# The rows' reciprocal roots on ScalarE and VectorE instead of GpSimd, with the planner's due places refitted

## Chip, cores and metric

The kernel runs on one core of a Trainium2 chip. The metric is the time of one execution on the device in microseconds; lower is better. A core has a matrix engine (TensorE, "PE" in the profile, with its weight loads as "PEld"), VectorE ("DVE"), ScalarE ("ACT"), GpSimd ("POOL") and a queue for transfers on SyncE ("SP"). Each engine works through its own list of instructions in order; semaphores hold an instruction until what it needs is there.

## What is computed

The input is x of shape 32 x 128 x 64 x 64 (images, channels, height, width) in fp32. Two layers follow each other:

```
# layer 0: group norm (32 groups), a convolution in a learned butterfly basis, and a residual
x = x + conv(_gn(x), weight, kd1, kd2, k11, k12, k21, k22)
# layer 1, on tokens: each image gives 4096 rows of 128 channels
t = _to_tokens(x)
t = t + attn(_ln_t(t), Wk, bk, Wv, bv)          # softmax over channels, one 128 x 128 matrix per image
t = t + moe(_ln_t(t), router_w, router_b, expert_w, expert_b)   # 8 experts, the 2 best per row
x = _from_tokens(t, x)

def _ln_t(v, eps=1e-5):
    m = jnp.mean(v, axis=-1, keepdims=True)
    s = jnp.var(v, axis=-1, keepdims=True)
    return (v - m) / jnp.sqrt(s + eps)
```

So every row is normalized twice in layer 1, and each time a reciprocal root of its variance is needed: 4096 rows an image, held as a 128 x 32 tile (row in the partition, 32 groups of 128 rows).

## The kernel before

The kernel has three parts. The first normalizes by groups and takes each image into the transform basis; the second mixes channels for each frequency; the third, which the change touches, takes one image after the other through the inverse transform, the attention and the experts.

In the third part three images are in work at once: image b is transformed back ("conv"), image b - 1 goes through both norms and the attention ("front"), and image b - 2 through the experts ("experts"). The steps of an image, by the keys that the code uses:

- conv: eight "w" on PE (L877, tile pu, from one PSUM buffer pair "cv" in use at a time), each emptied by two "wo" on ACT (L887, two copies each, into u); four "h" on PE (L899, py), each added to the image by "ho" on DVE (L907, y). The first two images use smaller pieces (L920, L939).
- front: "pt" transposes on PE (L1021), copied by "to" on ACT (L1026, tk); "sa" row statistics on DVE (L993, bs); "va" moments on DVE (L1003 to L1008, m); **"pwa"**, the power (L1013, m<-m,mhalf); "na" two small DVE operations (L1050, L1051); "xg" normalized rows on ACT (L1061); "pg" Gram matrix on PE (L1072); a short softmax chain ("gs", "pb", "sm", "pr", "sr", "sn", "pc", "prx", L1085 to L1124, with an Exp on ACT at L1107); "pp" products on PE (L1145), scaled by "at" on ACT (L1158, L1162) and added by "ad" on DVE (L1173); then "vb" moments, **"pwb"**, the second power, "lg" first half of the routing logits on DVE (L1204 to L1208), "nb" two small DVE operations (L1212, L1213), and the choice of experts on DVE ("l2", "f1" to "f4", "gt", L1218 to L1248) with one small Exp on ACT ("f5", L1239).
- experts: "xn" normalized rows on ACT (L1273), "px" transposes on PE (L1283), "xT" copies on ACT (L1289), 64 "pe" on PE (L1296), each weighed by "m" on DVE (L1307, tm), summed by sixteen "s" on POOL (L1332, L1333, L1335, five instructions each), transposed back by "st" on PE (L1342, po), copied by "so" on ACT (L1348) and stored. In the last image five of the sixteen sums are made on DVE instead (L1319).

The order of the instructions is written by a planner, `Plan`, when the kernel is built. Each step is added with its engine, an assumed duration in us, a due place, the steps that it needs, and the buffers that it takes and frees. The planner then plays the steps through: whenever an engine is free, it takes the ready step with the earliest due place whose buffers are free. The order that comes out is the order of the instructions on each engine; on the chip nothing is reordered. The due place of a step is its slot, 114 us an image, plus an entry of the table `SHIFT` for its key with the digits taken off ("w3" and "w0" are "w", "t1" is "t", "l2" is "l"):

```
        at += SHIFT.get(key.rstrip("0123456789_"), 0.0)
        made[b, key] = plan.add(
            engine, us, SLOT * at, run, [made[k] for k in names if k[0] >= 0], take, free, late
        )
```

Among the buffers are 3 for "pe" (PSUM), 3 for "tl" (PSUM, shared by the transposes and products), 1 for "cv", 2 each for the image x, xn, xT and tm.

The power is one GpSimd instruction: the variance plus epsilon, 128 x 32 values, to the power -1/2, with a tile of -0.5 as exponent (`mhalf`). It is planned with 5.5 us. The group norm of the first part has a power of its own (L349), which the change leaves as it is.

Of the kernel before, what the change touches and what calls it, by code (L numbers as in the profile page):

```python
# [11 lines left out]
AF = mybir.ActivationFunctionType  # L12
ALU = mybir.AluOpType
# [77 lines left out]
def kernel(  # L91
# [15 lines left out]
    nc = tc.nc  # L107
# [47 lines left out]
    mhalf = cp.tile([P, NT], F32, name="mhalf")  # L155
# [7 lines left out]
    with ExitStack() as ph1:  # L163
        pp = ph1.enter_context(tc.tile_pool(name="pp1", bufs=4, space=PSUM))
        xp = ph1.enter_context(tc.tile_pool(name="xp1", bufs=3))
        st = ph1.enter_context(tc.tile_pool(name="st1", bufs=1))
# [9 lines left out]
        def add(key, engine, us, at, run, after=(), take=(), free=(), late=0.0):  # L176
            after = [made[k] for k in after if k in made]
            if engine == "PE":
                after += on_pe[-1:]
            made[key] = plan.add(engine, us, SLOT * at, run, after, take, free, late)  # L180
            if engine == "PE":
                on_pe.append(made[key])
# [342 lines left out]
        for s in range(B + 2):  # L525
            if s == 0:
                norm(2)
            for g in range(4):
                at = s + 0.25 * g
# [36 lines left out]
    with ExitStack() as ph2:  # L566
# [146 lines left out]
        for w in range(n):  # L713
# [9 lines left out]
            for half in range(2):  # L723
                for t in range(4):
                    at = w + 0.5 * half + 0.125 * t
# [42 lines left out]
    st = ctx.enter_context(tc.tile_pool(name="st", bufs=1))  # L768
# [16 lines left out]
    xg = [ct.tile([P, 4, P], F32, name=f"xg{i}") for i in range(NG)]  # L785

    QX = P + 2 * NE
    prx = [ct.tile([P, QX], F32, name=f"prx{i}") for i in range(2)]
# [10 lines left out]
    def prepare():  # L799
# [24 lines left out]
    SLOT = 114.0  # L824

    SHIFT = {
        "ad": -0.15, "at": -0.25, "f": 0.71, "gs": -1.97, "gt": 0.71, "h": -0.24, "ho": -3.5, "kvp": 3.43,
        "kvq": -0.45, "l": 0.71, "lg": 3.61, "m": -0.32, "na": -1.87, "nb": -0.81, "pb": -1.97, "pc": -1.97,
        "pe": 0.16, "pg": -0.08, "pp": 0.19, "pr": -1.97, "prx": -1.97, "pt": -0.23, "pwa": -1.87, "pwb": 3.61,
        "px": 0.15, "r": -0.04, "s": 0.08, "sa": 1.29, "sm": -1.97, "sn": -1.97, "so": 2.13, "sr": -1.97,  # L830
        "st": 1.1, "t": -1.97, "to": 0.06, "va": -1.87, "vb": 3.61, "w": 0.28, "x": -0.68, "xT": -0.68,
        "xg": 0.21, "xn": 2.42,
    }
    made = {}

# [150 lines left out]
    def front(b):  # L986

        t = tk[b % 2]
        v = {}
# [5 lines left out]
        def moments(which):  # L995

            bs = v["bs"]
            even, odd = bs[:, :, 0, :], bs[:, :, 1, :]
            m2 = st.tile([P, 6, NT], F32, name=f"m2{which}_{b}", tag=f"m2{which}", bufs=2)
            total, diff, var, nmr, rstd, above = (m2[:, k, :] for k in range(6))  # L1000
            if which == 1:
                v["above"] = above
            nc.vector.tensor_add(total, even[:, :, 1], odd[:, :, 1])  # L1003
            nc.vector.tensor_sub(diff, even[:, :, 1], odd[:, :, 1])
            nc.vector.tensor_add(var, even[:, :, 2], odd[:, :, 2])
            nc.vector.tensor_mul(diff, diff, diff)
            nc.vector.tensor_scalar(var, var, 1.0 / P, LN_EPS, ALU.mult, ALU.add)
            nc.vector.scalar_tensor_tensor(var, diff, 0.25, var, ALU.mult, ALU.add)  # L1008
            v[which] = total, var, nmr, rstd

        def power(which):
            total, var, nmr, rstd = v[which]
            nc.gpsimd.tensor_tensor(rstd, var, mhalf, ALU.pow)  # L1013

        def turn(g):
            def run():
# [22 lines left out]
        s1 = b + 1  # L1039
        for g in range(8):  # L1040
            at = s1 + 0.016 * g
            add(b, f"pt{g}", "PE", 0.48, at, turn(g), [(b - 2, f"st{g}")] + [f"ho{k}" for k in range(4)], ("tl",))
            add(b, f"to{g}", "ACT", 0.55, at, turned(g), [f"pt{g}"], (), ("tl",))
            add(b, f"sa{g}", "DVE", 0.85, at, stats1(g), [f"to{g}"] + (["sa0"] if g else []))
        add(b, "va", "DVE", 1.7, s1 + 0.14, lambda: moments(1), [f"sa{g}" for g in range(8)])
        add(b, "pwa", "POOL", 5.5, s1 + 0.14, lambda: power(1), ["va"])

        def nmr1():
            total, var, nmr, rstd = v[1]
            nc.vector.scalar_tensor_tensor(nmr, total, -0.5, rstd, ALU.mult, ALU.mult)  # L1050
            nc.vector.tensor_scalar_add(v["above"], nmr, 1.0)  # L1051

        add(b, "na", "DVE", 0.9, s1 + 0.14, nmr1, ["pwa"])


        def norm(g):
# [21 lines left out]
        for g in range(8):  # L1078
            at = s1 + 0.26 + 0.016 * g
# [46 lines left out]
        at = s1 + 0.40  # L1126
# [50 lines left out]
        for j, lo in enumerate(range(0, NT, 3)):  # L1177
            m = min(3, NT - lo)
            at = s1 + 0.45 + 0.016 * j
# [28 lines left out]
            nc.vector.tensor_add(lg, lg, eq)  # L1208

        def nmr2():  # L1210
            total, var, nmr, rstd = v[2]
            nc.vector.scalar_tensor_tensor(nmr, total, -0.5, rstd, ALU.mult, ALU.mult)  # L1212
            nc.vector.tensor_scalar_add(nmr, nmr, 1.0)  # L1213
            tile_of["norm", b] = rstd, nmr
# [35 lines left out]

        at = s1 + 0.64
        add(b, "vb", "DVE", 1.7, at, lambda: moments(2), [f"ad{lo}" for lo in range(0, NT, 3)])
        add(b, "pwb", "POOL", 5.5, at, lambda: power(2), ["vb"])
        add(b, "lg", "DVE", 1.95, at, logits1, ["vb"])
        add(b, "nb", "DVE", 2.1, at + 0.1, nmr2, ["pwb", "lg"])
        add(b, "l2", "DVE", 1.95, at + 0.1, logits2, ["nb"], ("gate",))
        add(b, "f1", "DVE", 4.15, at + 0.1, lambda: first_max(0), ["l2"])
        add(b, "f2", "DVE", 0.4, at + 0.1, second, ["f1"])
# [123 lines left out]
    for b in range(B):  # L1382
        transfers(b)
        conv(b)
        front(b)
        experts(b)
# [37 lines left out]
def build(arrays):  # L1424
    import concourse.bacc as bacc

    nc = bacc.Bacc("TRN2", target_bir_lowering=False, num_devices=1)
    args = [
        nc.dram_tensor(k, a.shape, mybir.dt.from_np(a.dtype), kind="ExternalInput").ap() for k, a in arrays.items()
    ]  # L1430
    shape = arrays["in_x_dram"].shape
    args.append(nc.dram_tensor("out_0_dram", shape, F32, kind="ExternalOutput").ap())
    with tile.TileContext(nc) as tc:
        kernel(tc, *args)
    return nc
# [8 lines left out]
```

## Time and profile before

| | |
|---|---|
| Time, median of 3 runs | 6059.13 us (6056.47 to 6059.99) |
| Span of the profiled execution | 6062.4 us; no other time of that execution is recorded |
| First and second part | to about 2530 us |
| Third part | from about 2590 us to the end |
| Instructions | 219265 |
| Mean granted TensorE clock | 0.991 of full speed |

"Busy" is the time in which an engine has an instruction at work; register, branch and semaphore instructions and DMA issues are not counted. Matmuls are pipelined and their ends are modelled, so a matmul that is recorded with 0.592 us may follow the one before it by 0.43 us: on PE the starts are to be compared. The chain of work that ended last is followed back from the last instruction, at each step to what released it. A wait is put down to the releaser that came last. In the list of groups and in the timeline, the bracket at the end of a line is the time that the engine idled before the instruction, and what ended it. A matmul in fp32 that the code writes once appears as two instructions, a transpose as one.

### The profile page before, as it was taken

Reading aid. Unit: us, or ns where it says so; the run is one execution under the profiler, and the core shown is the slowest. Engines: PE = TensorE matmul, PEld = TensorE weight load, DVE = VectorE, ACT = ScalarE, POOL = GpSimd, SP = SyncE. Lnnn points to the kernel's source line nnn. Section 1 sums busy time; section 2 is a strip of 40 time slices with the busy share of each in tenths; the row PEclk is TensorE's granted clock in tenths of the full one; section 3 lists DMA queues with packets and bytes.
Section 4 is the critical chain, followed back from the end, with each engine's and each line's share of the span. In section 5 each row is a group of like instructions: output and inputs, shape, how many; then the busy total and the mean of one; then the engine's idle time right before and its main releaser. Section 6 shows DMA issues by size and latency. Waiting matters only on the chain.

```text
span 6062.4 us, 219265 instructions
## 1 busy us (share of the span) xinstructions
PE 5891.6 (97%) x95372; PEld 4677.6 (77%) x95372; DVE 4221.2 (70%) x7696; ACT 3756.5 (62%) x7057; POOL 4191.0 (69%) x3765
## 2 busy tenths in 40 slices
PE   7999999999999999889999999999999999999998
PEld 7999999999999999776666666666666666666654
DVE  5565545555555555448878787787878878787878
ACT  7666664555555555366667667666766766676663
POOL 2110006666666666428898898989989898998988
PEclk9999999999999999999999999999999999999999
DMA  6767666666666666632313222231322223132100
GB/s 200 238 224 237 234 214 193 172 173 172 172 174 171 171 171 172 160 107 77 92 56 102 67 88 81 72 97 57 101 68 84 84 64 104 57 97 71 65 27 28
DMA packets 555044, 756.74 MB, mean 125 GB/s; under 512 B 58592, under 2 KB 319712, under 8 KB 549984
## 3 DMA queue, kind: packets, MB, share of 16 engines
q1 hardware_dynamic: 551856, 738.76, 41.0%
q8 instruction: 749, 12.27, 0.9%
q0 software_dynamic: 896, 2.62, 0.1%
q14 instruction: 215, 1.76, 0.1%
q10 hardware_dynamic: 1328, 1.32, 0.1%
HBM read 406.93 MB, written 335.54 MB: 122 GB/s over the span
## 4 chain that ended last, share of the span: by engine, by line
PE 88%; ACT 7%; issue 2%; DVE 1%; POOL 1%; DMA 1%; SPq 0%; ACTq 0%; POOLq 0%; DVEq 0%
PE pe L1296 28%; PE m L654 17%; PE g L632 9%; PE pf L418 7%; PE pu L877 6%; PE pp L1145 4%; PE py L899 4%; PE pg L1072 4%; PE pv L396 3%; PE px L1283 2%; ACT xn L1273 2%; ACT u L887 2%; PE pz L373 1%; PE pt L1021 1%; ACT z L383 1%
## 5 line engine op out<-in xcount | busy, mean ns | idle before, releaser
L1296 PE MATMUL pe<-ew_sb,xT 128*128 128x512 f32 x4096 | 1948.4, 597 | 18.6 <-DVE tm L1307 15.1
L1307 DVE TENSOR_TENSOR tm<-pe,oh 128x512 f32<-128x512 f32 x2028 | 1346.6, 684 | 478.9 <-PE pe L1296 456.6
L1332 POOL TENSOR_TENSOR tm<-tm 128x512 f32<-128x512 f32 x1014 | 1285.0, 1284 | 202.6 <-DVE tm L1307 199.3
L1296 PEld LDWEIGHTS pe<-ew_sb,xT 128*128 128x128 f32 x4096 | 701.6, 191 | 523.4 <-issue 400.1
L643 DVE COPY f<-g 128x1024 f32<-128x1024 f32 x508 | 622.3, 1225 | 644.4 <-PE g L632 644.2
L654 PE MATMUL m<-f,s 128*64 128x64 f32 x32768 | 1068.9, 224 | 1.1 <-ACT f L643 0.8
L654 PEld LDWEIGHTS m<-f,s 128*64 128x64 f32 x32768 | 999.0, 138 | 62.4 <-issue 1.5
L600 POOL COPY s<-l 128x512 f32<-128x512 f32 x512 | 547.2, 1105 | 526.4 <-issue 509.7
L643 ACT COPY f<-g 128x1024 f32<-128x1024 f32 x508 | 514.7, 1013 | 556.4 <-PE g L632 530.1
L1335 POOL TENSOR_TENSOR tk<-tk,tm 128x256 f32<-128x256 f32 x1014 | 753.9, 743 | 79.5
L1333 POOL TENSOR_TENSOR tm<-tm 128x512 f32<-128x512 f32 x507 | 650.3, 1283 | 39.8
L887 ACT COPY u<-pu 64x512 f32<-64x512 f32 x960 | 556.3, 579 | 135.1 <-PE pu L877 121.6
L632 PE MATMUL g<-c,wst 9*128 9x128 f32 x16256 | 599.6, 283 | 1.7 <-issue 1.5
L632 PEld LDWEIGHTS g<-c,wst 9*128 9x128 f32 x16256 | 503.0, 186 | 36.2 <-issue 1.5
L349 POOL TENSOR_TENSOR grstd<-gms,mhalf 128x1 f32<-128x1 f32 x32 | 17.8, 555 | 737.8 <-DVE gms L345 737.8
L1158 ACT ACTIVATE pp<-pp,m 128x128 f32<-128x128 f32 x1024 | 440.9, 431 | 124.2 <-PE pp L1145 99.2
L602 POOL TENSOR_SCALAR s<-l 128x512 f32<-128x512 f32 x256 | 511.3, 1997 | 0.0
L877 PEld LDWEIGHTS pu<-qw,r 128*128 128x128 f32 x3840 | 455.1, 193 | 62.8 <-ACT u L887 49.0
L877 PE MATMUL pu<-qw,r 128*128 128x128 f32 x3840 | 475.8, 277 | 25.1 <-ACT u L887 25.1
L1289 ACT COPY xT<-px 128x512 f32<-128x512 f32 x256 | 150.2, 587 | 563.2 <-PE px L1283 560.1
L418 PE MATMUL pf<-ph,v 128*128 128x128 f32 x4096 | 491.2, 278 | 6.2 <-issue 1.4
L418 PEld LDWEIGHTS pf<-ph,v 128*128 128x128 f32 x4096 | 467.0, 192 | 16.0 <-ACT z L383 7.1
(169 smaller groups left out, 8569.6 us busy)
## 6 DMA issues: line engine op xcount, KB each, us to landing
xf<-f SPq DMA_DIRECT2D x512, 256.0 KB, 3.3
pf<-o SPq DMA_DIRECT2D x1024, 128.0 KB, 3.3
l<-xf SPq DMA_DIRECT2D x1012, 128.0 KB, 3.2
r<-pf SPq DMA_DIRECT2D x504, 256.0 KB, 4.7
x<-in_x_dram SPq DMA_DIRECT2D x256, 256.0 KB, 4.5
y<-in_x_dram SPq DMA_DIRECT2D x32, 2048.0 KB, 9.3
out_dram<-so SPq DMA_DIRECT2D x256, 256.0 KB, 2.2
tw<-in_tw_dram SPq DMA_DIRECT2D x6, 384.0 KB, 7.5
```

The costliest lines, as they stand in the source:

```text
L418: nc.tensor.matmul(pl[:, j * P : (j + 1) * P], vs[b][:, 8 * g + j, :], ph.rearrange("h r m -> h (r m)"), start=True, stop=True,)
L600: nc.gpsimd.tensor_copy(dst, src)
L632: nc.tensor.matmul(pg[g // 2][:, g % 2, m * P : (m + 1) * P], wst[rows, 16 * half + 4 * t + m, :], c[rows].rearrange("r h k -> r (h k)"), ...
L643: copy(f.rearrange("i m (g o) -> i m g o", g=2), tile_of["g", w, half, t][k].rearrange("i g (o m) -> i m g o", o=4))
L654: nc.tensor.matmul(ps[hh * n : (hh + 1) * n, q, :], s[:, h].rearrange("i k b -> i (k b)")[:, B * r : B * r + n], f[:, h, r, :], start=(r = ...
L877: nc.tensor.matmul(ps[:, k, :], rs[b, e][:, k * P : (k + 1) * P], qw.rearrange("w r m -> w (r m)"), start=True, stop=True,)
L887: nc.scalar.copy(u[r * n : (r + 1) * n, :, oh * n + 8 * e : oh * n + 8 * e + 8], ps[oh * n : (oh + 1) * n, :, r * n : (r + 1) * n].rearran ...
L1296: nc.tensor.matmul(ps, tile_of["xT", b, i // 4][:, i % 4, :], ew_sb[:, es, :].rearrange("d e c -> d (e c)"), start=True, stop=True,)
L1307: nc.vector.tensor_tensor(tile_of["tm", b, i // 2][:, i % 2, es, :], tile_of.pop(("pe", b, i, half)).rearrange("p (e c) -> p e c", c=P), t ...
L1332: nc.gpsimd.tensor_tensor(tm[:, k, 0:4, :], tm[:, k, 0:4, :], tm[:, k, 4:8, :], ALU.add)
L1333: nc.gpsimd.tensor_tensor(tm[:, :, 0:2, :], tm[:, :, 0:2, :], tm[:, :, 2:4, :], ALU.add)
L1335: nc.gpsimd.tensor_tensor(t[:, lo : lo + 2, :], t[:, lo : lo + 2, :], tm[:, :, m, :], ALU.add)
```

## The change

Both powers of the third part leave GpSimd. In their place ScalarE takes the natural logarithm of the variance and then the exponential of -0.5 times it, and VectorE makes one Newton step on the result, three instructions, at the head of "na" and "nb". The planner's steps "pwa" and "pwb" become ACT steps of 0.55 us, "na" goes from 0.9 to 1.4 us and "nb" from 2.1 to 2.6. Every entry of SHIFT is new; two keys that no step uses are gone, and "wo" is added.

```
@@ SHIFT
-        "ad": -0.15, "at": -0.25, "f": 0.71, "gs": -1.97, "gt": 0.71, "h": -0.24, "ho": -3.5, "kvp": 3.43,
-        "kvq": -0.45, "l": 0.71, "lg": 3.61, "m": -0.32, "na": -1.87, "nb": -0.81, "pb": -1.97, "pc": -1.97,
-        "pe": 0.16, "pg": -0.08, "pp": 0.19, "pr": -1.97, "prx": -1.97, "pt": -0.23, "pwa": -1.87, "pwb": 3.61,
-        "px": 0.15, "r": -0.04, "s": 0.08, "sa": 1.29, "sm": -1.97, "sn": -1.97, "so": 2.13, "sr": -1.97,
-        "st": 1.1, "t": -1.97, "to": 0.06, "va": -1.87, "vb": 3.61, "w": 0.28, "x": -0.68, "xT": -0.68,
-        "xg": 0.21, "xn": 2.42,
+        "ad": -4.220, "at": -1.623, "f": 1.979, "gs": -2.122, "gt": 1.288, "h": -0.225, "ho": -2.066,
+        "l": -0.694, "lg": 13.929, "m": -3.037, "na": 2.809, "nb": 3.903, "pb": -3.699, "pc": -8.262,
+        "pe": 0.110, "pg": -1.062, "pp": 0.179, "pr": -1.382, "prx": -2.690, "pt": -0.071, "pwa": 3.358,
+        "pwb": -2.233, "px": 0.135, "r": 3.879, "s": 10.318, "sa": 8.276, "sm": -7.752, "sn": -3.975,
+        "so": -2.291, "sr": 8.801, "st": 0.395, "t": -1.530, "to": -11.017, "va": -4.512, "vb": 4.281,
+        "w": 6.698, "wo": 0.030, "x": -4.067, "xT": -6.105, "xg": 0.748, "xn": 3.218,
@@ front
         def power(which):
             total, var, nmr, rstd = v[which]
-            nc.gpsimd.tensor_tensor(rstd, var, mhalf, ALU.pow)
+            nc.scalar.activation(rstd, var, AF.Ln)
+            nc.scalar.activation(rstd, rstd, AF.Exp, scale=-0.5)
+
+        def newton(which):
+            total, var, nmr, rstd = v[which]
+            nc.vector.scalar_tensor_tensor(var, var, -0.5, rstd, ALU.mult, ALU.mult)
+            nc.vector.tensor_tensor(var, var, rstd, ALU.mult)
+            nc.vector.scalar_tensor_tensor(rstd, var, 1.5, rstd, ALU.add, ALU.mult)
...
-        add(b, "pwa", "POOL", 5.5, s1 + 0.14, lambda: power(1), ["va"])
+        add(b, "pwa", "ACT", 0.55, s1 + 0.14, lambda: power(1), ["va"])
         def nmr1():
+            newton(1)
...
-        add(b, "na", "DVE", 0.9, s1 + 0.14, nmr1, ["pwa"])
+        add(b, "na", "DVE", 1.4, s1 + 0.14, nmr1, ["pwa"])
...
         def nmr2():
+            newton(2)
...
-        add(b, "pwb", "POOL", 5.5, at, lambda: power(2), ["vb"])
+        add(b, "pwb", "ACT", 0.55, at, lambda: power(2), ["vb"])
...
-        add(b, "nb", "DVE", 2.1, at + 0.1, nmr2, ["pwb", "lg"])
+        add(b, "nb", "DVE", 2.6, at + 0.1, nmr2, ["pwb", "lg"])
```

## The prediction

> **What bounds the kernel now.** The profile page comes first: the busy shares, and the chain of work that ended last.
>
> ```profile
> PE 5891.6 (97%) x95372; PEld 4677.6 (77%) x95372; DVE 4221.2 (70%) x7696; ACT 3756.5 (62%) x7057; POOL 4191.0 (69%) x3765
> ...
> PE 88%; ACT 7%; issue 2%; DVE 1%; POOL 1%; DMA 1%; SPq 0%; ACTq 0%; POOLq 0%; DVEq 0%
> ```
>
> TensorE carries 88% of the chain and GpSimd 1%. These are means over stages, so next come the stretches of the last part, cut at the first transform matmul of an image (L899), which returns every 106.37 us: (5825.49 - 4017.26) / 17.
>
> ```profile
> core 0: us, PE busy (x) PEld busy (x) DVE busy (x) ACT busy (x) POOL busy (x), PEclk, DMA share, GB/s
> 2847.10:2953.50 106.40, 105.05 (x744) 71.82 (x743) 85.47 (x189) 72.91 (x168) 95.28 (x83) 1.00 0.26 80
> 5719.10:5825.50 106.40, 105.06 (x746) 71.85 (x747) 85.48 (x189) 73.05 (x168) 95.26 (x83) 1.00 0.11 41
> 5825.50:5931.90 106.40, 94.08 (x447) 56.68 (x448) 85.51 (x196) 58.95 (x148) 93.71 (x82) 0.94 0.05 20
> 5931.90:6062.00 130.10, 109.28 (x336) 53.02 (x334) 110.19 (x224) 39.95 (x94) 113.81 (x105) 0.94 0.09 33
> ```
>
> From 2847 to 5825 there are 28 equal slots, one image each: PE busy 105.05 of 106.40, POOL 95.3, DVE 85.5, ACT 73. Behind them lies a tail of 237 us in which PE has gaps. The waits of PE in the 28 slots are only two kinds, and the timeline of one slot shows each:
>
> ```profile
> PE pt L1021 <- ACT tk L1026: 22.2, 28, 0.8
> PE pu L877 <- ACT u L887: 14.9, 28, 0.5
> ```
>
> ```profile
> 4062.45 2.05 PE L877 MATMUL pu<-qw,r 128*128 128x128 f32 x16 [0.53 <-ACT u L887]
> ...
> 4079.67 0.66 PE L1021 MATMUL pt<-ident,y 128*128 128x128 f32 x4 [0.79 <-ACT tk L1026]
> ```
>
> So a slot holds 0.53 + 0.79 = 1.32 us of PE waiting, both times for a copy on ACT: what GpSimd does is not what PE waits for. Last, the power itself, by its line, and the tail's chain:
>
> ```profile
> L1013 POOL TENSOR_TENSOR m<-m,mhalf x64: 5427/5440/5616, 2614.1 to 5956.9; 128x32 f32<-128x32 f32 x64
> ```
>
> ```profile
> 5889.70 5.45 POOL m L1013
> ...
> 5956.94 5.41 POOL m L1013
> ```
>
> 64 powers of 5.44 us, two an image; only the last image's two lie on the chain, 10.86 us together.
>
> **The change part by part.** *Removed:* two powers a slot, 10.9 us of POOL. In the 28 slots that is POOL going from 95.3 to 84.4 of 106.4 while PE stays at 105; worth 0 there, since POOL itself waits for DVE (162.6 us on tm in the 28 slots). Covered by PE's own work; were the cover gone, POOL would still have 11 us of idle a slot.
>
> *Added on ACT:* per power one Ln and one Exp on 128x32. The nearest row is the Exp of the gate (L1239), same shape, 0.233 us, so 0.47 us a power (bounds from the 128x48 copy, 0.198, and the 128x128 Exp, 0.367: 0.40 to 0.73). Beyond that stands the question of tables. The trace has one load:
>
> ```profile
> 10.30 1.28 ACT L360 ACT_TABLE_LOAD   x1 [10.30 <-DVE gbs L319]
> ```
>
> It stands before the first Identity at 10.30 us; the first Exp comes at 2640.7 us (L1107) without another, so Identity, Copy and Exp share what was loaded. No row has an Ln. Low bound: Ln is in it too, or one later load serves all: nothing per image. High bound: Ln and Exp are never active together, and each power then loads twice, four loads an image, 4 x 1.283 = 5.13 us. I take the high bound: the one load was placed in front of the function that first needed it, long before any Exp, and a load placed the same way in front of an Ln has only that Ln in view; it is a choice, not shown. A power then costs 2 x 1.283 + 0.47 = 3.03 us, where the planner reserves 0.55: 2.48 us late. ACT rises from 72.9 to 72.9 + 2 x 3.03 = 79.0 of 106.4 and does not become the bound.
>
> The Trainium skill, "ScalarE: Activation LUTs", section on table sets, speaks against my choice: it names a set that holds both exp and ln and counts one load for ln followed by exp. By it the sum would be the faster rival's below. The same page, on what a load costs, adds a drain and states 2.66 us for every switch; no row here shows that drain. By that price, as an estimate, a power would be 5.8 us, and the sum of this forecast would be some 77 us higher.
>
> *Who waits for a late power.* Two places a slot. (1) On ACT, the copies behind the power are 2.48 us later than planned. The trace shows no cover from 4056.9 to 4084, where ACT runs nearly without a break and PE already waits twice; outside it ACT has gaps of 1.0 to 5.4 us (1.42, 1.05, 3.05, 5.44 in the slot at 4017). The first power of an image can fall in a gap (in this trace it comes at 4087, when ACT idles 5.44 us), the second (4048) just ahead of the dense stretch. One exposed power at half: 1.24 us a slot. (2) "na" on DVE now begins with Newton, which waits for the Exp. DVE is in order: behind it are queued the tm multiplies (L1307) that empty the three "pe" buffers, and PE waits for those. The planner lets DVE reach it after 0.55 us, it is ready after 3.03. Cover: PE fills a buffer in 0.86 us, so it runs on for one to three of them, 0.9 to 2.6; I take half of 2.48 again, 1.24 us. "nb" is different: it also waits for "lg", placed after everything else on DVE by its new +13.929, so its power has time; 0 (if that cover were gone, another 1.24).
>
> A longer gap costs more than its length here: after 2.58 us without work the 12 matmuls at 5985.37 took 6.97 us, not 12 x 0.43 = 5.16 (granted clock 0.94 in that stretch), while after 1.51 at 5860.09 two took 1.13, nearly the usual 1.10. A delay laid bare whole thus costs 2.48 + 1.8 = 4.3 us. That belongs to the upper end.
>
> *Added on DVE:* six Newton instructions a slot. Small SBUF operations cost 0.18 to 0.20 us when POOL leaves them alone (L1008: 0.192 median) and up to 1.28 when they begin behind a POOL operation (L1212: 1.283 median, about a POOL sum's 1.284). I take 0.72 for the first (mean of the medians 0.19 of L1008, 0.69 of L1050, 1.28 of L1212), 0.19 for two more: 1.1 us; the nmr instruction that pays now comes later and cheaper, so some 0.57 net, 1.15 a slot. DVE has 20.9 us idle; 0 on the path, 1.15 if bare.
>
> *Moved:* all due places. DMA issue: x and r only shift on SP, which has nothing else to do but out's stores, and PE waits for no DMA in the 28 slots; 0. On ACT the copies "to", "xT", "so" go earlier relative to the others; on DVE "ad" and "m" (which empty PSUM) go first and "sa", "vb", "lg" become fillers; on PE "w" goes from +0.28 to +6.70 slots: last of all, a filler too. An order can win at most the 1.32 us of waiting per slot, since PE is full otherwise. What it can lose is open. I credit half, 0.66.
>
> *The tail:* of the two powers on the chain, 5.43 each, each becomes 3.03 + 1.1 = 4.13: -1.3 x 2 = -2.6 us.
>
> **Sum.** Per slot 1.24 + 1.24 - 0.66 = +1.82; times 28 = +51.0; tail -2.6. On the profiled span: 6062.4 + 48.4 = 6110.8 us. The span stands 3.3 us over the median of the runs (6059.13), the profiled execution having no other time on record; taken off: 6107.5, said as 6107.
>
> **The rivals.** *Faster: no loads between Ln and Exp.* A power is then 0.47, inside the planner's 0.55, and nothing is late. The order wins 0.66 to 1.32 a slot (18.5 to 37 us), the tail 2 x (5.43 - 0.47 - 1.1) = 7.7: between 6059.1 - 26.2 = 6033 and 6014. It decides whenever bare delay per slot stays under 0.66 us. For it: both PE waits are order-made, and POOL becomes looser. Against: the two functions alternate 64 times. Chance 0.27, time 6033.
>
> *Slower by the order itself.* "w" comes last on PE and has a single PSUM buffer "cv", emptied by two pairs of ACT copies of 1.18 us each, 2.36 in all; eight a slot. Today other matmuls lie between. If two of eight are pushed to where PE has nothing else, 2 x 2.36 = 4.7 us a slot, 132 us in all: 6191. It decides from 1.4 us a slot on (0.66 of credit, 0.27 of tail, 0.43 for the 12 us below), 7% of these copies' 18.9 us. Against it: the planner fills gaps by readiness. Chance 0.13.
>
> *It does nothing that counts.* The powers were off the path, the loads fall into ACT's 33 us of idle, the order trades evenly: 6059. Chance 0.05.
>
> **How the numbers follow.** The forecast has 0.55. Its own range: net 0.3 a slot (most delay covered) to 4 a slot, 6065 to 6169. The whole range: below, the faster rival with both waits gone, 6014; above, one delay bare with the slow clock and the other at half, 4.3 + 1.24 - 0.66 = 4.9 a slot, +137, or the order, 6191. I give 6015 to 6190, leaving about 0.07 below and 0.11 above. A change within 0.2% (12 us) is about what cannot be told from none here. Faster 0.27, same 0.05, slower 0.55 + 0.13 = 0.68.
>
> **What would show it.** Right: ACT_TABLE_LOAD some 129 times, ACT near 79 a slot, POOL near 84, period near 108.2 us, PE waits behind ACT copies and behind DVE tm, DVE waiting for ACT before the Newton. Wrong: one or two loads in all, or a period of 105.0 to 105.7 with loads fully in ACT's gaps; POOL still at 95; or PE waiting mainly before pu, which would be the order and not the loads.

## The result, and the profile after

The changed kernel takes 6226.9 us (median of 4 runs, 6225.02 to 6229.56) against 6058.3: ratio 1.0277, 95% interval 1.0263 to 1.0291. It is slower by 2.8%, as forecast in sign, but by 169 us and not 48: above the stated range. The profiled execution's span is 6227.3 us, 164.9 more than before. The page's busy shares and chain:

```profile
PE 5932.4 (95%) x95372; PEld 4708.2 (76%) x95372; DVE 4368.7 (70%) x7888; ACT 3929.2 (63%) x7313; POOL 3850.1 (62%) x3701
...
PE 74%; DVE 12%; ACT 10%; issue 3%; DMA 1%; POOL 1%; SPq 0%; ACTq 0%; POOLq 0%; DVEq 0%
```

Before, PE had 88% of the chain and DVE 1%. Now DVE has 12%. DVE is not fuller as a share of the span (70% in both), so the chain says that something on DVE comes at the wrong time.

Where the 165 us lie is read from the transform matmuls (L899), whose fourth group ends an image's way back. From image 3 to image 31 it takes 5987.76 - 2859.13 = 3128.6 us, 111.74 a slot, against 106.37: 5.37 us more in each of 28 slots, 150.3 in all. Ahead of them the third image is 12.0 us later than before (its slot takes 123.9 us), behind them the tail is 2.6 us longer. So it is a matter of the equal slots. Two of them, the first 6.6 us behind PE's longest wait in the first of the two, and PE's waits between 3000 and 5700 us (24 slots):

```profile
3976.60:4088.89 112.29, 106.85 (x744) 73.54 (x744) 90.19 (x196) 78.63 (x176) 84.48 (x81) 0.98 0.23 76
4009.40:4016.00 6.60, 6.56 (x32) 5.57 (x33) 4.45 (x10) 5.10 (x11) 4.74 (x4) 0.74 0.36 130
4046.95:4157.65 110.70, 105.25 (x744) 71.87 (x743) 90.60 (x196) 78.31 (x177) 84.49 (x81) 1.00 0.23 77
```

```profile
PE pe L1306 <- DVE tm L1317: 117.4, 73, 2.8
PE pu L877 <- ACT u L887: 13.0, 24, 0.5
```

ACT stands at 78.3 and POOL at 84.5, close to what was worked out (79.0 and 84.4); DVE at 90.6, where 86.6 was expected. PE waits 130.4 / 24.2 = 5.4 us a slot where it waited 1.32, and nearly all of it for a tm multiply on DVE (L1317), a wait that the kernel before did not have in its slots at all.

So about 4 of the 5.37 us a slot are added waiting. The rest, some 1.4 us, is PE being slower: it is busy 106.4 us a slot over the 28 slots, where it was 105.0 before. The granted clock is 0.98 in 20 of the 28 slots and 1.00 in the other eight, while in the kernel before all 28 have 1.00. In the first slot above it is 0.74 in the 6.6 us right behind the 2.81 us wait, and PE is busy 1.6 us longer than in the second. Why a wait of this length costs clock in one slot and not in another, no run shows.

The largest of the waits, 2.81 us, on PE and then on DVE in the same stretch:

```profile
4004.68 1.95 PE L877 MATMUL pu<-qw,r 128*128 128x128 f32 x16
4009.44 1.13 PE L1306 MATMUL pe<-ew_sb,xT 128*128 128x512 f32 x2 [2.81 <-DVE tm L1317]
```

```profile
4001.20 0.43 DVE L1003 TENSOR_TENSOR m<-bs 128x32 f32<-128x32 f32 x1
...
4002.36 1.27 DVE L1006 TENSOR_TENSOR m<-m 128x32 f32<-128x32 f32 x1
4003.56 1.30 DVE L1007 TENSOR_SCALAR m<-m 128x32 f32<-128x32 f32 x1
...
4005.00 1.26 DVE L1213 SCALAR_TENSOR_TENSOR m<-m,m 128x32 f32<-128x32 f32 x1
...
4008.36 0.43 DVE L1217 TENSOR_TENSOR lg<-lg,eq 128x256 f32<-128x256 f32 x1
4008.70 0.68 DVE L1317 TENSOR_TENSOR tm<-pe,oh 128x512 f32<-128x512 f32 x1
```

From 4001.20 to 4008.70 DVE does the second moments and at once the first logits, eleven small operations in 7.5 us, planned with 1.7 + 1.95 = 3.65. No tm runs in that time, all three pe buffers stay full, and PE stands still with transposes and products queued behind the waiting matmul. POOL in the same stretch:

```profile
4002.32 2.50 POOL L1342 TENSOR_TENSOR tm<-tm 128x512 f32<-128x512 f32 x2
4004.90 1.31 POOL L1343 TENSOR_TENSOR tm<-tm 128x512 f32<-128x512 f32 x1
4006.29 1.75 POOL L1345 TENSOR_TENSOR tk<-tk,tm 128x256 f32<-128x256 f32 x2
```

The two sums at 4002.32 meet about 4003.57 and end at 4004.82. DVE's L1006 ends at 4003.63, L1007 at 4004.86, L1213 at 4006.26 and POOL's next sum at 4006.21. Each of these DVE operations ends within 0.06 us behind the end of a POOL instruction. Now the same moments before, and POOL beside them:

```profile
4047.57 0.18 DVE L1006 TENSOR_TENSOR m<-m 128x32 f32<-128x32 f32 x1
4047.68 0.18 DVE L1007 TENSOR_SCALAR m<-m 128x32 f32<-128x32 f32 x1
...
4050.35 0.42 DVE L1206 TENSOR_TENSOR lg<-lg,lq 128x256 f32<-128x256 f32 x1
```

```profile
4048.17 5.44 POOL L1013 TENSOR_TENSOR m<-m,mhalf 128x32 f32<-128x32 f32 x1 [0.59 <-DVE m L1008]
```

Before, the power was next in POOL's list: POOL idled 0.59 us until the moments were done, and then spent 5.44 us on the power, while DVE's logits ran at 0.42 each. The power was a pause in POOL's sums, at the very place where DVE has its small operations. Over the whole run moments and first logits (L1003 to L1008 and the five lines of the logits) take 179.8 us before and 372.3 after, 5.6 and 11.6 us an image.

The table loads are there as taken, two a power and 129 in all with the first:

```profile
L1013 ACT ACT_TABLE_LOAD x64 | 82.1, 1283 | 1.1
L1014 ACT ACT_TABLE_LOAD x64 | 82.1, 1283 | 1.1
```

### The profile page after: what moved, and what is told of

It is laid out like the page before. It is cut to its first block, busy times and chain, and to the rows that moved or that the text cites. A ratio compares the mean times of both kernels' runs of the same rounds, so it can differ in the third digit from the quotient of the medians.

```text
span 6227.3 us, 219848 instructions
## 1 busy us (share of the span) xinstructions
PE 5932.4 (95%) x95372; PEld 4708.2 (76%) x95372; DVE 4368.7 (70%) x7888; ACT 3929.2 (63%) x7313; POOL 3850.1 (62%) x3701
## 3 DMA queue, kind: packets, MB, share of 16 engines
q10 hardware_dynamic: 1328, 1.32, 0.1%
## 4 chain that ended last, share of the span: by engine, by line
PE 74%; DVE 12%; ACT 10%; issue 3%; DMA 1%; POOL 1%; SPq 0%; ACTq 0%; POOLq 0%; DVEq 0%
PE pe L1306 21%; PE m L654 16%; PE g L632 9%; PE pf L418 6%; PE pu L877 4%; PE pg L1081 4%; ACT pp L1167 3%; DVE tm L1317 3%; PE pv L396 3%; ACT u L887 2%; PE pp L1154 2%; PE py L899 2%; PE po L1352 1%; PE pz L373 1%; ACT z L383 1%
## 5 line engine op out<-in xcount | busy, mean ns | idle before, releaser
L1306 PE MATMUL pe<-ew_sb,xT 128*128 128x512 f32 x4096 | 1977.5, 603 | 166.8 <-DVE tm L1317 163.9
L1317 DVE TENSOR_TENSOR tm<-pe,oh 128x512 f32<-128x512 f32 x2028 | 1330.0, 684 | 401.7 <-PE pe L1306 375.9
L1070 ACT ACTIVATE xg<-tk,m 128x128 f32<-128x128 f32 x1024 | 398.1, 480 | 151.5 <-DVE m L1060 151.5
```

Source lines behind the costliest of these rows:

```text
L1306: nc.tensor.matmul(ps, tile_of["xT", b, i // 4][:, i % 4, :], ew_sb[:, es, :].rearrange("d e c -> d (e c)"), start=True, stop=True,)
L1317: nc.vector.tensor_tensor(tile_of["tm", b, i // 2][:, i % 2, es, :], tile_of.pop(("pe", b, i, half)).rearrange("p (e c) -> p e c", c=P), t ...
```

## The experiments

Theory A: the loads. ACT is held longer than planned and PE waits for it. Theory B: DVE. Its small operations stand in blocks, and wait for POOL, which has lost its pause. Each run is given as a ratio to the kernel before on the same chip; the changed kernel has 1.0277. A tenth of a percent is 6 us. The columns that the text uses, from each run's profile: the mean slot, moments and first logits per image on DVE, and PE's waits behind tm from 3000 to 5700 us.

| run | ratio (95%) | slot us | moments, logits us | PE behind tm us |
|---|---|---|---|---|
| before | 1 | 106.37 | 5.6 | 0 |
| changed | 1.0277 (1.0263 to 1.0291) | 111.74 | 11.6 | 117.4 |
| e1 one load | 1.0274 (1.0258 to 1.0289) | 111.8 | 11.7 | 118.7 |
| e2 due places alone | 1.0488 (1.0472 to 1.0503) | unequal | 7.2 | 42.8 |
| e3 move alone | 1.0169 (1.0152 to 1.0186) | 109.7 | 10.6 | 80.6 |
| e4 no Newton | 1.0225 (1.0210 to 1.0240) | 110.8 | 11.7 | 108.8 |
| e5 lg one tm later | 1.0174 (1.0159 to 1.0189) | 109.7 | 11.2 | 49.9 |
| e6 pause, new table | 1.0183 (1.0168 to 1.0198) | 109.6 | 7.8 | 61.3 |
| e7 pause, old table | 1.0157 (1.0140 to 1.0174) | 109.9 | 8.0 | 57.4 |
| e8 POOL half | 0.9955 (0.9940 to 0.9969) | 105.7 | 6.0 | 0 |
| e9 before, POOL half | 0.9975 (0.9965 to 0.9984) | 106.37 | 4.3 | 0 |
| e10 POOL short | 1.0251 (1.0234 to 1.0268) | 111.2 | 11.6 | 108.5 |
| e11 new table mended | 1.0075 (1.0060 to 1.0090) | 107.8 | 11.1 | 39.8 |
| e12 old table mended | 1.0101 (1.0086 to 1.0116) | 108.8 | 9.9 | 61.7 |

### e1: one load

```
     make_identity(nc, ident)
+    nc.scalar.preload_act_table_set("natural_log_exp_and_others")
```

> One table set that serves Ln and Exp is loaded once at the start, so the 128 table loads of the third part are gone; order and all else as in the changed kernel. Theory A (the loads: ACT is held 2.6 us longer than planned, twice an image, and PE waits for that): most of the 5.4 us a slot comes back, 6075 to 6110 us. Theory B (DVE: its small operations stand in long blocks beside a POOL that never pauses, and PE waits for its buffers to be emptied): the loads lie beside DVE's block, under 1 us a slot comes back, 6195 to 6227 us.

The profile of this run has one load in all, and the wait of PE as it was:

```profile
L125 ACT ACT_TABLE_LOAD x1 | 1.3, 1283 | 0.8 <-PEq L1438 0.8
```

```profile
PE pe L1307 <- DVE tm L1318: 118.7, 73, 2.8
```

128 loads, 164 us of ACT, are gone and the ratio does not move. Theory A falls. The changed kernel's timeline shows why the loads are free, here at the second power of an image: the first of the two does not wait for the moments, it is issued at 4001.60 while ACT would wait for them anyway (2.23 us more, until 4005.12), and the second ends at 4006.64, while DVE is busy with the logits until 4008.70 and comes to the Newton step at 4009.30. At the next image's first power the Exp ends at 4051.82, and DVE, with tm multiplies and an image addition in front, comes to Newton at 4054.17.

### e2 and e3: the due places alone, the move alone

e2 is the kernel before with the new SHIFT table; e3 is the changed kernel with the old one.

> The kernel before with the new due places only; the powers stay on POOL. Theory A: the order is harmless, 6040 to 6070 us. Theory B by order alone (vb and lg in one block on DVE): 6180 to 6230 us. Theory B by POOL's pause (while POOL is at the power, 5.4 us, DVE's small operations take 0.2 to 0.4 us and not up to 1.3): the block shrinks from 7.5 to some 3 us and the PE wait of 2.8 us nearly goes, 6060 to 6110 us.

> The changed kernel with the old due places: Ln, Exp, Newton on ACT and DVE, planned at the new costs. Theory A: as slow as the change, 6190 to 6250 us. Theory B by order alone: 6055 to 6080 us. Theory B by POOL's pause: the moments take 3 to 4 us again and not 1.8, but vb and lg stand apart, so PE waits less than in the changed kernel: 6100 to 6180 us.

e3 gives 1.0169: the moved powers, in the order that the planner makes of them, cost 1.7%, inside what theory B with the pause expected. Its slot has PE waits of 1.90 us behind moments that POOL's sums slow down, and up to 1.51 behind such logits. e2, 1.0488, was missed by all: no theory expected it above the change itself. In its profile PE waits most for ACT's copies of the inverse transform (77.1 us from 3000 to 5700, 3.9 at the longest) and POOL waits up to 13.6 us for DVE ahead of a power. The table and the durations belong together; the planner played through with one and not the other gives another order altogether, so the two parts don't add up (4.9 and 1.7 against 2.8), and e2 tells nothing of what the table does in the change.

### e4: no Newton

```
         def nmr1():
-            newton(1)
...
         def nmr2():
-            newton(2)
```

> The changed kernel without the three Newton instructions of each power (the root is left at the accuracy of Ln and Exp); the planned costs are kept, so the order is the same. Theory A: DVE has room, no change, 6220 to 6230 us. Theory B: the Newton steps stand in DVE's blocks at 0.6 to 1.9 us each, of which the short PE wait after the first moments (0.45 us) is made: 0.4 to 1 us a slot less, 6195 to 6215 us.

This kernel leaves the root at the accuracy of Ln and Exp. Beside e1, on the same chip, it is 0.5% faster, some 30 us: near the upper end of theory B's 12 to 32, and against A's zero. Newton's 76 us of DVE were not free. The short waits behind the first moments are gone (49 waits behind tm, not 73), the one of 2.8 us stays. Part of the gain is the clock: 13 of the 28 slots have 0.98, not 20.

### e5: lg one tm later

In the order that the planner gives, the step lg is held back on DVE until one more tm multiply has been emitted (images 2 to 30); nothing else moves.

```
+        plan.late = {made[b, k] for b in range(2, B - 1) for k in ('lg',)}
+        plan.marks = {i for k, i in made.items() if k[1][0] == "m"}
...
-        for i in order:
+        for i in self.moved(order):
             ops[i][3]()
```

> The changed kernel; on DVE alone the step lg of every image is emitted behind the next tm multiply, so that vb and lg no longer stand in one block; all other engines keep their order. If the PE wait of 2.8 us a slot comes from this block: it nearly goes, 2 to 2.8 us a slot less, 6150 to 6175 us. If PE is late for another reason: 6215 to 6230 us.

```profile
PE pu L896 <- ACT u L906: 50.7, 49, 1.5
PE pe L1325 <- DVE tm L1336: 49.9, 50, 1.7
```

One multiply between two blocks brings 2.1 us a slot, 1.0%. The wait of 2.8 us behind tm is gone; those of up to 1.7 us were there before. The granted clock is 1.00 in all 28 slots. PE waits longer for ACT's copies instead (50.7 us, 13.0 in the changed kernel), which takes back part of the gain. The small operations are nearly as slow as in the changed kernel (11.2 us an image for 11.6): it is their standing in one block that this run takes away, and it shows that the block made the wait.

### e6 and e7: a pause on POOL again

```
             nc.scalar.activation(rstd, rstd, AF.Exp, scale=-0.5)
+            idle = st.tile([P, NT], F32, name=f"idle{which}_{b}", tag="idle", bufs=2)
+            nc.gpsimd.tensor_tensor(idle, v["diff"], mhalf, ALU.pow)
```

> The changed kernel with a power on POOL beside Ln and Exp, at the same place, its result unused: 5.4 us more work for POOL, twice an image, in which POOL makes no sums. If POOL's pause let DVE's small operations run freely: moments and first logits together (372 us in the changed kernel, 180 us in the one before) fall to 200 to 260 us and the time to 6130 to 6190 us, although work is added. If POOL's presence is not the cause: 6225 to 6260 us.

> The same unused power on POOL, added to the moved roots with the old due places (6168 us without it). If the pause is the cause: nearly the time of the kernel before, 6075 to 6115 us. If the loss is in Ln, Exp, Newton or the planned order: 6160 to 6190 us.

e6 adds 64 instructions of 5.44 us to POOL whose result nobody reads, and the kernel becomes 0.9% faster, about 57 us. Its third operation of the logits (L1218), against the changed kernel's (L1215):

```profile
L1218 DVE TENSOR_TENSOR lg<-lg,lq x32: 424/425/426, 2687.2 to 6067.1; 128x256 f32<-128x256 f32 x32
```

```profile
L1215 DVE TENSOR_TENSOR lg<-lg,lq x32: 424/829/1378, 2680.5 to 6119.5; 128x256 f32<-128x256 f32 x32
```

In e6 all 32 of them begin while POOL is at the unused power, and none takes more than 0.426 us; without it the median is 0.829. That is the pause shown by itself. It gives back about a third of the 169 us. The wait of 2.8 us is gone and the granted clock is 1.00 in all slots, but the added work has a price: DVE now waits 168 us (3000 to 5700 us) for POOL to free a tm buffer, a wait that the changed kernel does not have.

e7 missed: its 6164 us lie in the range named for the other explanation, not for the pause. With the old table the logits go down in the same way (moments and logits 8.0 from 10.6) and the 1.5 us wait behind them is gone in 15 of 25 slots and shorter (1.0 us) in ten, but the ratio stays within e3's interval and the slot, 109.9 from 109.7, is no shorter. Its profile shows two parts of the reason. At the first power of an image POOL is behind with its sums and comes to the pause at 4035.14, when the moments (4030.53 to 4034.4) are over; they were slow again, and the 1.90 us wait stayed. And right behind that wait the granted clock falls to 0.74 in 11 of 28 slots, against 4 in e3. So with the old table it is not shown that the lost pause is what the moved powers cost.

### e8 and e9: POOL's instructions at half length, after and before

```
-                    nc.gpsimd.tensor_tensor(tm[:, k, 0:4, :], tm[:, k, 0:4, :], tm[:, k, 4:8, :], ALU.add)
+                    nc.gpsimd.tensor_tensor(tm[:, k, 0:4, 0:64], tm[:, k, 0:4, 0:64], tm[:, k, 4:8, 0:64], ALU.add)
```

and so for the other sums: both kernels leave out half of every sum, so they time the work and don't compute the whole result.

> The changed kernel with every POOL sum of the experts made for 64 of 128 columns (the rest of the sum is left out): POOL's instructions are half as long, the order is the same. If DVE waits behind POOL's instructions one by one: moments and first logits fall from 372 to some 250 to 300 us and the time to 6140 to 6190 us. If not: POOL was at 76% and nobody waited for it, 6215 to 6230 us.

> The kernel before with the halved POOL sums of the run above (64 of 128 columns, the rest left out). If halving took away a loss that the change had brought: little here, since PE waits for ACT alone in this kernel, 6040 to 6068 us. If halving helps any kernel of this kind: 5880 to 6000 us, and the run above says nothing about the change.

e8's only wait of PE in the slots:

```profile
PE pu L877 <- ACT u L887: 20.8, 50, 0.6
```

and its fourth operation of the moments, with the changed kernel's behind it:

```profile
L1006 DVE TENSOR_TENSOR m<-m x64: 175/188/735, 2616.4 to 5935.4; 128x32 f32<-128x32 f32 x64
```

```profile
L1006 DVE TENSOR_TENSOR m<-m x64: 179/1276/1291, 2610.9 to 6116.0; 128x32 f32<-128x32 f32 x64
```

The longest falls from 1.291 to 0.735 us, with POOL's 512-column sum from 1.286 to 0.733 us: DVE waits for the end of the POOL instruction that is running. All waits behind tm are gone, the granted clock is 1.00 in all slots, and 6.0 us a slot come back, more than any theory expected. e9 is the control: the kernel before has no such wait, and its slots stay at 106.37; its 15 us lie, by its profile, in the tail, which POOL does set in part (236.9 to 221.8 us). So halving POOL's sums brings 6.02 us a slot in the changed kernel (111.74 to 105.72) and nothing in the one before: that is what DVE's waiting for POOL costs, with PE's waits and the lower clock behind them. Without that cost the changed kernel would be a little the faster, by 0.65 us a slot; no kernel that makes the whole sum shows this.

### e10: the same sums in shorter instructions

Each 512-column sum is made as two over 256.

> The changed kernel with each POOL sum over 512 columns cut into two over 256, three such per pair of rows; the whole sum is made, POOL's work grows by some 0.6 us a pair (128x256 takes 0.743, half of 128x512's 1.286 is 0.643). If a DVE operation waits for the end of one POOL instruction: waits of 0.7 and not 1.3, moments and first logits from 372 to 260 to 310 us, time 6130 to 6190 us. If it waits for POOL's work as a whole: no gain or worse, 6225 to 6270 us.

```profile
L1006 DVE TENSOR_TENSOR m<-m x64: 180/735/745, 2615.0 to 6105.7; 128x32 f32<-128x32 f32 x64
```

A single wait does shrink, to 0.745 us at most, but more operations have one (484 of 544, where it was 334), and moments and logits still take 11.6 us an image. 1.0251 against 1.0277: no gain that the intervals separate. This points to how long POOL is at sums while DVE has its small operations, not to the length of one instruction. Neither expectation describes this.

### e11 and e12: the mends together

e11 has e1, e4, e5 and e10 on the changed kernel, e12 has e1, e4 and e10 with the old table.

> The changed kernel with what the runs point to: POOL's sums cut in two, lg one tm later, no Newton, one table load. The gains of the single runs were 24 (Newton) and 55 us (lg) and would be 40 to 90 (cut): 6070 to 6130 us; under the kernel before only if they add up and more.

> The moved roots with the old due places, POOL's sums cut in two, no Newton, one table load. PE's two waits there were 1.9 and 1.5 us a slot behind contended DVE operations; with halved waits: 6075 to 6130 us. If it comes under the kernel before, POOL's relief is worth something after all: below 6060 us.

1.0075 and 1.0101: the first within what was expected, the second a microsecond above it (6131.13 us), and neither under the kernel before. The power on POOL stays the fastest of all complete versions tried.

## Why the prediction was right and wrong

**Removing the powers, "worth 0": the step that failed.** It looked for who waits for POOL's power, and nobody did. It did not ask who runs better while POOL is at it. The rows were on the page: L1212 with a median of 1.283 against L1008 with 0.192, and they were even read, as a price for Newton alone. The same price falls on the other small DVE operations with two inputs in SBUF that now meet POOL's sums: 6.0 us an image more on DVE for moments and logits alone, and 6.0 us a slot in the end (e8); the two numbers are alike, but measure different things. Of the loss a pause on POOL gives back about a third (e6) and taking the block apart 2.1 us a slot (e5); that the two add up is not shown. The bound of this term should have reached below nothing.

**Slower: right by luck.** The two terms that made the forecast slower are late powers, and both measured 0. PE does wait behind DVE's tm, as was said, but for moments and logits, not for a Newton step that waits for the Exp: in the 28 slots DVE never waits for ACT there.

**DVE's 20.9 us of idle as cover: wrong.** 90.6 of 110.7 still leaves idle. But the wait comes from 7.5 us without a tm, not from DVE being full; PE's three buffers cover about 2.6 us of that, and transposes and products some 3 us more (4003.38 to 4006.63).

**The loads: count right, price wrong.** Two a power, as taken; ACT at 78.3 for 79.0. The two terms of 1.24 us for a late power measured 0 (e1): the first load runs while ACT waits for the moments, and on DVE other work stands ahead of Newton.

**A gap that costs more than its length: right, and left out of the sum.** The prediction read it from the tail and kept it for the upper end. It came in 20 of 28 slots and is some 1.4 of the 5.37 us.

**The order, credited with 0.66.** Where POOL holds DVE up less, the whole change brings 0.65 (e8 against e9), and PE's wait for ACT's tk copy, 0.79 us, is gone. That it agrees so closely is luck: 0.66 was half of a bound. But the same order puts vb and lg back to back, and e5 shows 2.1 us a slot for that. That "vb" and "lg" become fillers was said; that two fillers fall into one block was not worked out.

**Newton: 0, or 1.15 a slot if bare.** Measured at about 30 us, 0.95 a slot (e4 against the changed kernel, 110.8 from 111.7); its busy time, 1.2 us a power, was forecast at 1.1.

**The tail and the range.** -2.6 forecast, +2.6 measured; the third image's slot, 17.5 us longer than before, was not foreseen and not studied. The range's top came from loads and from the copies behind "w", which were not the cause, so 6190 was not an upper bound of anything that happened.

**The rivals.** "No loads between Ln and Exp" was to be decided by late powers; e1 made that case true and the time stayed. "Slower by the order itself" named the copies behind "w"; PE waits for them as before (13.0 us from 3000 to 5700, 13.3 before). The page "ScalarE: Activation LUTs" of the Trainium skill, in its section on table sets, is right that one set serves both, as e1's single load shows; the changed kernel alternates between two sets all the same. Its 2.66 us for a switch with a drain is not seen here: the Exp begins at 4006.66, 0.02 us after a load that ended at 4006.64.

A rule that speaks against this change was there and was not weighed. The Trainium skill, "Advanced Engine Details and Errata", section on GpSimd, says that the Pool engine shares a read and a write interface with DVE and conflicts with DVE instructions that have two SBUF inputs or use a two-port mode. The rows agree: operations with two inputs in SBUF slow down, while the tm multiply, with one input in PSUM, has 0.684 us in both kernels, and reductions and reciprocals, which have one input, keep their time beside a sum (L1255: 0.352 to 0.355 us). L1007, with one input, was slowed too (1.30 us); whether by a two-port mode no run shows. Here the conflict lasts until the end of POOL's instruction.

## What to carry to other kernels

Before taking work off an engine that is not the bound, look at what other engines do while it is at that work: here a slow instruction was the quiet time in which another engine's small operations ran at 0.2 and not 1.3 us. In an in-order queue, measure the longest stretch without the operation that empties the bottleneck's buffers, not the queue's idle time. And due places fitted to one set of durations don't carry over to another: the same table with the old powers cost 4.9%.

## What the runs showed of the hardware that was not expected

- A DVE operation with two inputs in SBUF that begins beside a POOL sum lasts until that sum ends: up to 1.291 us with sums of 1.286, up to 0.735 with sums of 0.733 (L1006). Some that begin within 0.05 us of the sum's start escape (L1020 at 2936.2 us, 0.19 us long). Reductions and reciprocals, with one input, don't (L1255: 0.352 to 0.355 us, 29 of 32 of them beside a sum).
- POOL's power does not do this: for its 5.44 us DVE's moments and logits run at 0.17 to 0.43 us.
- A table load is issued ahead of the wait of the function that needs it: 4001.60, with the function at 4005.12. One of two loads a power hides in that wait.
- A wait of PE can cost clock behind it: the granted clock of the next 6.6 us was 0.74 behind waits of 2.5 to 2.8 us in 20 of 28 slots of the changed kernel and 13 of 28 of e4, behind 1.9 us in 4 of 28 (e3) and 11 of 28 (e7), and 1.00 behind all waits up to 1.7 us (e5, e6, e11).
